# A ternary FFN on Trainium2: the first half group of W1 on ScalarE's queue, quarters for the gathered weights, and two chunks crosswise

## The chip, the cores and the metric

One Trainium2 chip, one of its cores. A core has TensorE (PE, with its weight loads shown apart as PEld), VectorE (DVE), ScalarE (ACT), GpSimd (POOL) and SyncE (SP). They run side by side, each takes its own instructions in order, and they wait for each other by semaphores. DMA queues move data between the device memory and the on-chip memory. The metric is the device time of one execution in microseconds; lower is better.

## The reference

An input `x` of 128 samples, 64 channels and 512 positions is multiplied, sample by sample, by a 64x64 matrix drawn from a table of 200; the result goes through a two-layer network whose weights are made ternary; the output is quantized to 4 bits with one scale for the whole tensor and added to `x`.

```python
def ternarize(W, threshold):                 # threshold 0.05
    absW = jnp.abs(W)
    delta = threshold * jnp.max(absW)
    mask = absW > delta
    n = jnp.maximum(jnp.sum(mask), 1)
    alpha = jnp.sum(jnp.where(mask, absW, 0.0)) / n
    Wt = alpha * jnp.sign(W) * mask
    return W + jax.lax.stop_gradient(Wt - W)

w = weights[conditions]                      # (128, 64, 64) of (200, 64, 64)
c = jnp.einsum('bct,bcd->bdt', x, w)         # "mix": (128, 64, 512)
h = ternary_linear(c, W1, b1)                # 512 -> 2048
h = jax.nn.gelu(h, approximate=False)
y = ternary_linear(h, W2, b2)                # 2048 -> 512
scale = jnp.max(jnp.abs(y)) / 7 + 1e-8
q = jnp.clip(jnp.round(y / scale), -7, 7) * scale
out = x + q
```

Two things set the order at the start: W1's threshold `delta` needs the maximum over the whole of W1 (4 MB), and nothing of layer 1 can be multiplied before it is known.

## The kernel before

**Tiling.** The 128 samples form 16 blocks of 8 samples. A block is four pairs (`PAIRS`), and a pair of samples fills 128 partitions with its 2 x 64 channels; `BLK` = 512 columns of a block are four pairs of 128. Layer 1 has 16 chunks of 128 hidden units (`NH`, index `hc`), layer 2 sums over the same chunks. W1 is held in four groups (`NG`) of four chunks (`GH`), 1 MB each (128 partitions x 2048 float32), in the tiles `nat1[0]` to `nat1[3]`, `nat` in the profile.

**Two parts for each number.** An activation is split into a rounded part in float32r and a rest in float16 (k = 0 and k = 1), and a matrix product runs over both. The ternary weights are held narrow (`terns`, bfloat16) and are widened to float32r by GpSimd (`widen1`, `wf<-terns`) for the first part.

**Program order.** The wrapper `InOrder` (line 36, to which the profile puts almost all instructions) keeps every engine's instructions in the order in which the program writes them. So the order of calls in the source is each engine's queue, and an instruction that waits holds up all that stands behind it on its engine.

**The start, in the order of the source.**

- SP issues all loads: the condition numbers (`first`, 32 KB), W1's pieces by `PIECES` (groups 0 and 1 whole, group 2 in two halves, group 3 in a half and two quarters), x of block 0 in two halves (`load_x(0)`), then b1, W2 (`nat2`), and b2. VectorE makes row numbers (`rows`) of the condition numbers, and GpSimd gathers the table's rows with them: `fetch(n, j)` gathers for block n and pair j into `wg`.
- PE runs 46 matmuls on constants (`idle`) while the loads come in.
- For each piece of W1 VectorE takes the maximum of the absolute values (`top<-nat`). ScalarE makes for groups 0 to 2 the signs (`sign1`) and, in place, the absolute values (`abs1`).
- `place_all(0)`: GpSimd copies all four gathered pairs into the block diagonal matrix `diag` by two instructions, one for each half of the partitions. `place(n, j)` does the same for one pair; later blocks use it.
- `thresholds`: VectorE takes the maximum over the pieces and spreads it, PE turns it across the partitions (`tops_delta_w`), VectorE takes the maximum again and makes `delta1`.
- `mix0(j)` for the four pairs: PE multiplies x by `diag` (`pc<-diag,xt`, eight passes for a pair). `hi0(j)`: ScalarE rounds the result. `lo0(j)`: VectorE makes the rest.
- `mask1`, `signed1` (VectorE): mask and ternary weights of a group; group 0 is done in two halves of two chunks each. Between them stand the four `lo0`.
- `early(hc)`: layer 1's matmuls of block 0 and chunk hc. Chunk 0 is done in two halves of the columns (pairs 0 and 1, then pairs 2 and 3), k = 0 before k = 1 in each; chunk 1 whole. Each chunk has a PSUM bank of its own (`slot`).
- `count1`: PE counts the masks for alpha; `above1` (ScalarE) sums what lies above the threshold.

The passage around the change reads

```python
    mask1(0, parts1[0])
    signed1(0, parts1[0])
    for j in range(2):
        fetch(1, j)
    widen1(0, 0)
    widen1(0, 1)
    for j in range(2, PAIRS):
        fetch(1, j)
    lo0(0)
    ...
    early(0)
    early(1)
    mask1(0, parts1[1])
    signed1(0, parts1[1])
    widen1(0, 2)
    widen1(0, 3)
    abs1(3)
```

After it come, for GpSimd, `widen1(0, 4)`, `widen1(0, 5)`, `place_all(1)`, which reads the gathers of block 1, and `widen1(0, 6)` and further; for PE `count1(0)`, `early(2)`, `early(3)`, the counts of the other groups, `early(4)` and further. From there on block 0's layer 1 and layer 2 run, then blocks 1 to 15.

Of the kernel before, what the change touches and what calls it, by code (L numbers as in the profile page):

```python
# [15 lines left out]
AF = mybir.ActivationFunctionType  # L16
# [23 lines left out]
def tile_cond_ternary_ffn(  # L40
# [12 lines left out]
    pe, act, dve, pool, sp = (  # L53
        InOrder(tc, e) for e in (nc.tensor, nc.scalar, nc.vector, nc.gpsimd, nc.sync)
    )
    B, C, T = x.shape
# [4 lines left out]
    PAIRS = 4  # L61
    BLK = PAIRS * P
    NB = B // (2 * PAIRS)
    NG = 4
    GH = NH // NG
# [44 lines left out]

    nat1, nat2 = [], []

    PIECES = [[slice(0, GH)], [slice(0, GH)], [slice(0, 2), slice(2, GH)]]
    PIECES.append([slice(0, 2), slice(2, 3), slice(3, GH)])
    W1f = W1.rearrange("p k c h -> p k (c h)")
    for g in range(NG):
        w = big.tile([P, GH, T], F32, tag="big", name=f"nat1_{g}")
        for ks in PIECES[g]:
            sp.dma_start(out=w[:, ks, :], in_=W1f[:, g * GH :, :][:, ks, :])
        nat1.append(w)  # L120
    x_next = load_x(0)
    b1t = const.tile([P, NH], F32)
# [1 line left out]
    for g in range(NG):  # L124
        w = big.tile([P, GH, T], F32, tag="big", name=f"nat2_{g}")
# [30 lines left out]
    def half_of(h):  # L156
        return slice(h * C, (h + 1) * C)
# [8 lines left out]
    def fetch(n, j):  # L166

        pair = n * PAIRS + j
        if j == 0:
            gathered[n] = gather.tile([P, PAIRS, D], F32, tag="wg", name=f"wg_{n}")  # L170
        pool.indirect_dma_start(
            out=gathered[n][:, j, :],
            out_offset=None,
            in_=table,
            in_offset=bass.IndirectOffsetOnAxis(ap=rows[:, pair : pair + 1], axis=0),
        )

    def place(n, j):
        for h in range(2):
            out = diag[half_of(h), j, h * D : (h + 1) * D]  # L180
            pool.tensor_scalar(out, gathered[n][half_of(h), j, :], UP, None, ALU.mult)

    def place_all(n):
        for h in range(2):
            out = diag[half_of(h), :, h * D : (h + 1) * D]
            pool.tensor_scalar(out, gathered[n][half_of(h)], UP, None, ALU.mult)
# [3 lines left out]
    def parts(n):  # L190
        return [
            big.tile([P, NT, BLK], t, tag="big", name=f"x{k}_{n}")
            for k, t in enumerate((F32R, F16))
        ]
# [6 lines left out]
    def pair_of(xt, j):  # L201
        return xt[j // 2][:, j % 2, :]

    def mix(xp, j, pc):

        for c in range(NT):
            pe.matmul(
                out=pc[:, c, :],
                lhsT=xp[:, c * P : (c + 1) * P],
                rhs=diag[:, j, :],  # L210
                start=True,
                stop=True,
            )
# [7 lines left out]
    def spread(top1, out, wide_top, space=ps_c, tag="pc"):  # L221

        dve.tensor_copy(wide_top, top1.to_broadcast([P, P]))
        tops = space.tile([P, P], F32, tag=tag, name=f"tops_{out.name}")
        pe.transpose(tops, wide_top, ident_f)
        return tops

    def thresholds(w, top, room):

        top1 = const.tile([P, 1], F32, name=f"top1_{w}")  # L230
        dve.tensor_reduce(top1, top, AX.X, ALU.max)
        delta = const.tile([P, 1], F32, name=f"delta_{w}")
        tops = spread(top1, delta, room)
        yield
        dve.tensor_reduce(delta, tops, AX.X, ALU.max)
        dve.tensor_scalar(delta, delta, THRESHOLD, None, ALU.mult)
        minus = const.tile([P, 1], F32, name=f"minus_{w}")
        dve.tensor_scalar(minus, delta, -1.0, None, ALU.mult)
        yield delta, minus
# [9 lines left out]
    def flat(w):  # L249
        return w.rearrange("p a b -> p (a b)")  # L250


    signs = [big.tile([P, 2, WCH], BF16, tag="big", name=f"signs_{i}") for i in range(2)]
# [3 lines left out]
    above = junk[:, 0, :]  # L257
    top_1 = const.tile([P, sum(map(len, PIECES))], F32)
    sums1 = const.tile([P, NG], F32)

    def group1(tiles, g):
        return tiles[g // 2][:, g % 2, :]

    def sign1(g):
        act.activation(group1(signs, g), flat(nat1[g]), AF.Sign)

    mags = nat1[: NG - 1]

    def abs1(g):

        if g == NG - 1:
            mags.append(big.tile([P, GH, T], F32, tag="big", name="mag"))
        act.activation(flat(mags[g]), flat(nat1[g]), AF.Abs)


    idle = ps_h.tile([P, T], F32, tag="ph", name="idle")
# [6 lines left out]
    for g in range(NG):  # L283
        for ks in PIECES[g]:
            dve.tensor_reduce(
                top_1[:, at : at + 1],
                flat(nat1[g][:, ks, :]),
                AX.X,
                ALU.max,
                apply_absolute_value=True,  # L290
            )
            at += 1
        if g < NG - 1:
            sign1(g)
            abs1(g)
    place_all(0)
    two_next = parts(0)
    pcs = []

    def mix0(j):  # L300
        home, tag = [(ps_c, "pc"), (ps_h, "ph"), (ps_y, "py0"), (ps_y, "py1")][j]
        pc = home.tile([P, NT, P], F32, tag=tag, name=f"pc_0_{j}")
        mix(pair_of(x_next, j), j, pc)
        pcs.append(pc)
# [4 lines left out]
    def lo0(j):  # L309
        part = slice(j * P, (j + 1) * P)  # L310
        dve.tensor_tensor(
            two_next[1][:, :, part], pcs[j], two_next[0][:, :, part], ALU.subtract
        )

    find = thresholds("w1", top_1, first[:, 3, :P])
    next(find)
    delta1, minus1 = next(find)
    for j in range(PAIRS):
        mix0(j)
    hi0(0)  # L320
    hi0(1)
# [1 line left out]
    def mask1(g, part=slice(0, WCH)):  # L323

        dve.tensor_scalar(
            group1(masks, g)[:, part], flat(mags[g])[:, part], delta1, None, ALU.is_gt
        )

    def signed1(g, part=slice(0, WCH)):
        dve.tensor_tensor(  # L330
            group1(terns, g)[:, part],
            group1(masks, g)[:, part],
            group1(signs, g)[:, part],
            ALU.mult,
        )
# [33 lines left out]
    def widen1(n, hc):  # L369

        if n == 0:
            w = w1f[hc % 4]
            g, i = divmod(hc, GH)
            pool.tensor_copy(flat(w), group1(terns, g)[:, i * T : (i + 1) * T])
        else:
            w = w1f[hc % 2]
            pool.tensor_copy(flat(w), w1t[:, hc])
        wide1[n, hc] = w
# [13 lines left out]
    halves = slice(0, HALF), slice(HALF, BLK)  # L392
# [10 lines left out]
                    stop=(c == NT - 1 and k == 1),  # L403
                )

    def layer1_0(n, hc, ph, part=slice(0, BLK), between={}):
        g, i = divmod(hc, GH)
        narrow = group1(terns, g)[:, i * T : (i + 1) * T].rearrange("p (c h) -> p c h", c=NT)
        for k in range(2):
            w = narrow if k else wide1[n, hc]  # L410
            for c in range(NT):
                between.get((k, c), lambda: None)()
                pe.matmul(
                    out=ph,
                    lhsT=w[:, c, :],
                    rhs=cond[n][k][:, c, part],
                    start=(c == 0 and k == 0),
                    stop=(c == NT - 1 and k == 1),
                )
# [80 lines left out]
    ring = [t[:, i, :] for t in rings for i in range(2)]  # L500
    ring += [quarter.tile([P, BLK], F32, tag="quarter", name=f"ring_{i}") for i in (10, 11)]

    def early(hc, between={}):

        slot = (hc + 4) % 6
        if slot < 2:
            ph = ps_h.tile([P, BLK], F32, tag="ph", name=f"ph_0_{hc}")
        else:
            ph = ps_y.tile([P, BLK], F32, tag=f"py{slot - 2}", name=f"ph_0_{hc}")
        for part in halves if hc == 0 else [slice(0, BLK)]:  # L510
            layer1_0(0, hc, ph[:, part], part, between)
        waiting[hc] = ph

    def early_bend(hc):
        if hc % 2 == 0:
            pairs0[hc // 2] = big.tile([P, 2, 2, BLK], F32R, tag="big", name=f"h_{hc}")
        two = [pairs0[hc // 2][:, hc % 2, k, :] for k in range(2)]
        on_pool = hc in (0, 2, 4, 6)
        bend(0, hc, waiting.pop(hc), two, ring[hc % len(ring)], pool if on_pool else None)
# [79 lines left out]

    mask1(0, parts1[0])  # L600
    signed1(0, parts1[0])
    for j in range(2):
        fetch(1, j)
    widen1(0, 0)
    widen1(0, 1)
    for j in range(2, PAIRS):
        fetch(1, j)
    lo0(0)
    lo0(1)
# [1 line left out]
    hi0(3)  # L611
    lo0(2)
    lo0(3)
    early(0)
    early(1)
    mask1(0, parts1[1])
    signed1(0, parts1[1])
    widen1(0, 2)
    widen1(0, 3)
    abs1(3)  # L620
    for g in range(NG):
        above1(g)
# [66 lines left out]
    for hc in range(NH - LAG):  # L689
# [13 lines left out]
        if hc in (5, 7, 9, 11):  # L703
            j = (hc - 5) // 2
# [191 lines left out]
    order = [*range(AWAY, NB - 2), *range(AWAY), NB - 2]  # L896
# [212 lines left out]
    while s < len(steps):  # L1109
        n, hc = steps[s]  # L1110
# [10 lines left out]
    n = NB - 1  # L1121
# [108 lines left out]
```

## Time and profile before

| | |
|---|---|
| median of 3 runs | 963.38 us (963.26 to 963.51) |
| the profiled execution | 963.14 us |
| its span, first to last instruction | 961.4 us |
| PE busy | 949.9 us (99%) |
| VectorE, ScalarE, GpSimd busy | 708.3, 637.0, 705.3 us |
| granted TensorE clock | 0.999 |
| read from and written to the device memory | 46.44 and 32.51 MB |

A PE that is busy for 99% of the span includes the 46 matmuls on constants (2.96 to 14.91 us), which compute nothing that is needed. A view by line says little here, because all instructions stand at line 36; the names of the tiles tell them apart. The first 45 us, in order of time, are what bears on the change. The landing of a transfer is its issue time plus the time from issue to landing that the view of a tile gives: the numbers land at 2.5 us, group 0 at 6.0, group 1 at 8.5, x's first half at 15.7.

### The profile page before, as it was taken

To read this page: it belongs to the slowest core of one execution; us is meant where nothing else is said; L and a number is where in the kernel's file an instruction comes from. 1 tells how busy PE (TensorE), PEld (TensorE's weight loads), DVE (VectorE), ACT (ScalarE), POOL (GpSimd) and SP (SyncE) were. 2 spreads that over 40 slices of the span, in tenths; PEclk is the share of its full clock that TensorE was granted. 3 is DMA by queue.
4 is the path that set the end of the run, shared out by engine and by line. 5 is a ranking of instruction groups with operands and counts; after the bars stand their busy time and mean duration, and the time that the engine had idled before them with its cause. 6 is when DMAs were issued, how large, how long until landed. Compare 5 with 4: busy or idle time off the path is not lost.

```text
span 961.4 us, 17574 instructions
## 1 busy us (share of the span) xinstructions
PE 949.9 (99%) x6072; PEld 739.3 (77%) x6072; DVE 708.3 (74%) x1239; ACT 637.0 (66%) x1148; POOL 705.3 (73%) x1060
## 2 busy tenths in 40 slices
PE   8999999999999999999999999999999999999997
PEld 4687667888788788788878778788878878878784
DVE  7999766666676766666676676666667798888986
ACT  7995446656656666665666656666565777878784
POOL 6866867677686776767767686776767879788872
PEclk9999999999999999999999999999999999999999
DMA  9301011110111100111010111100131184575751
GB/s 359 103 23 47 14 33 49 32 61 15 35 49 34 60 24 25 52 41 49 25 70 15 34 50 33 59 25 25 49 121 60 47 305 172 186 239 170 277 204 61
DMA packets 33195, 80.11 MB, mean 83 GB/s; under 512 B 3792, under 2 KB 3792, under 8 KB 30160
## 3 DMA queue, kind: packets, MB, share of 16 engines
q1 hardware_dynamic: 31056, 76.86, 22.7%
q0 software_dynamic: 2048, 2.10, 0.7%
q8 instruction: 49, 0.80, 0.3%
q14 instruction: 42, 0.34, 0.1%
HBM read 46.44 MB, written 32.51 MB: 82 GB/s over the span
## 4 chain that ended last, share of the span: by engine, by line
PE 96%; DVE 2%; DMA 1%; ACT 1%; issue 0%; POOL 0%; SPq 0%; ACTq 0%
PE py L36 47%; PE xy L36 22%; PE z L36 16%; PE pc L36 6%; PE ph L36 6%; DVE top L36 1%; DMA nat<-in_L_ffn_W 1%; DVE xt L36 0%; DVE y_last L36 0%; ACT diag L36 0%; POOL wf L36 0%; PE number L36 0%; DVE y L36 0%; ACT h L36 0%; ACT ring L36 0%
## 5 line engine op out<-in xcount | busy, mean ns | idle before, releaser
L36 PE MATMUL py<-wf,h 128*128 128x512 f32 x1088 | 316.5, 416 | 0.7 <-DVE y L36 0.6
L36 POOL CAST wf<-w2t 128x512 fp32r<-128x512 fp8e4 x240 | 229.6, 977 | 105.2 <-PE py L36 102.1
L36 POOL CAST wf<-sums 128x256 fp32r<-128x256 fp8e4 (+1 forms) x336 | 183.0, 550 | 86.1 <-PE xy L36 82.3
L36 PEld LDWEIGHTS py<-wf,h 128*128 128x128 f32 x1088 | 196.6, 189 | 45.1 <-POOL wf L36 0.8
L36 DVE SCALAR_TENSOR_TENSOR low_parts<-ring,h 128x512 f16<-128x512 f32 x228 | 202.1, 924 | 39.3 <-ACT h L36 39.3
L36 PE MATMUL py<-w2t,low_parts 128*128 128x512 fp8e4 x920 | 218.6, 379 | 0.0
L36 ACT ACTIVATE ring<-ring,b1t,alpha_up 128x512 f32<-128x512 f32 x216 | 175.2, 818 | 58.8 <-DVE ring L36 53.9
L36 DVE TENSOR_TENSOR ring<-xy,ring 128x256 f32<-128x256 f32 x216 | 119.8, 555 | 119.3 <-PE xy L36 119.3
L36 ACT COPY ring<-xy 128x256 f32<-128x256 f32 x216 | 80.5, 373 | 171.7 <-PE xy L36 171.2
L36 PEld LDWEIGHTS <-low_parts 128*128 128x128 f16 x920 | 89.6, 97 | 84.5 <-issue 0.3
L36 ACT ACTIVATE h<-ring 128x512 fp32r<-128x512 f32 x232 | 133.9, 626 | 0.6
L36 POOL CAST wf<-w1t 128x256 fp32r<-128x256 fp8e4 (+1 forms) x240 | 131.3, 563 | 2.5 <-PE xy L36 0.3
L36 PE MATMUL xy<-xb,wf 128*128 128x256 f32 x448 | 98.8, 302 | 0.0
L36 PE MATMUL xy<-xt,wf 128*128 128x256 f32 x448 | 88.1, 277 | 0.1
L36 PE MATMUL xy<-xl,sums 128*128 128x256 f16 x448 | 87.9, 278 | 0.0
L36 PE MATMUL xy<-xl,w1t 128*128 128x256 f16 x448 | 86.8, 275 | 0.0
L36 PE MATMUL z<-xl,sums 128*128 128x256 f16 x448 | 85.5, 273 | 0.0
L36 PEld LDWEIGHTS xy<-xt,wf 128*128 128x128 f32 x448 | 76.2, 188 | 10.2 <-issue 0.2
L36 PEld LDWEIGHTS xy<-xb,wf 128*128 128x128 f32 x448 | 75.9, 189 | 10.2
L36 PEld LDWEIGHTS <-sums 128*128 128x128 fp8e4 x896 | 69.3, 97 | 14.8
L36 POOL DMA_INDIRECT wg<-in_L_cond_weights,rows x64 | 63.9, 998 | 18.2 <-issue 8.6
L36 PEld LDWEIGHTS <-w1t 128*128 128x128 fp8e4 x736 | 61.6, 98 | 18.0 <-issue 4.3
(134 smaller groups left out, 1349.3 us busy)
## 6 DMA issues: line engine op xcount, KB each, us to landing
xt<-in_x SPq DMA_DIRECT2D x36, 512.0 KB, 5.6
y_dram<-y SPq DMA_DIRECT2D x15, 1024.0 KB, 4.3
out<-xt SPq DMA_DIRECT2D x30, 512.0 KB, 3.4
x_quarters<-in_x SPq DMA_DIRECT2D x56, 256.0 KB, 2.7
nat<-in_L_ffn_W SPq DMA_DIRECT2D x6, 1024.0 KB, 10.2
y_back<-y_dram SPq DMA_DIRECT2D x2, 1024.0 KB, 7.4
nat<-in_L_ffn_W SPq DMA_DIRECT2D x3, 512.0 KB, 8.7
wg<-in_L_cond_weights,rows POOLq DMA_INDIRECT x64, 2.5
```

Of the source, the lines that this page charges most:

```text
L36: return lambda *args, **kw: self._tc.keep_in_program_order(make(*args, **kw))
```

## The change

- W1's group 0 comes in two halves. The first is issued from ScalarE's queue, as ScalarE's first instruction; SP issues the second after the numbers. VectorE's maximum, `sign1` and `abs1` of group 0 are done by halves (both signs, then both absolute values).
- `place_all(0)` becomes four `place(0, j)`: eight instructions, two behind each gather, for two.
- `mix0(0)` moves ahead of the threshold's transpose on PE; pairs 1 to 3 stay behind it.
- `early(0)` and `early(1)` become `early_two()`: chunk 1 also in two halves of the columns, and the eight sets of four matmuls in a crosswise order, in which chunk 0's second half, k = 1, comes after chunk 1's first half. `early` no longer splits chunk 0, and the choice of the bank is a function of its own.
- On GpSimd one `fetch` of block 1 instead of two stands ahead of the first two widenings, two stand behind them, and `fetch(1, 3)` moves behind `widen1(0, 3)`.

```diff
-    PIECES = [[slice(0, GH)], [slice(0, GH)], [slice(0, 2), slice(2, GH)]]
+    PIECES = [[slice(0, 2), slice(2, GH)], [slice(0, GH)], [slice(0, 2), slice(2, GH)]]
...
-        for ks in PIECES[g]:
-            sp.dma_start(out=w[:, ks, :], in_=W1f[:, g * GH :, :][:, ks, :])
+        for i, ks in enumerate(PIECES[g]):
+            queue = act if g == 0 and i == 0 else sp
+            queue.dma_start(out=w[:, ks, :], in_=W1f[:, g * GH :, :][:, ks, :])
...
-            sign1(g)
-            abs1(g)
-    place_all(0)
+            pieces = PIECES[g] if g == 0 else [slice(0, GH)]
+            for ks in pieces:
+                sign1(g, ks)
+            for ks in pieces:
+                abs1(g, ks)
+    for j in range(PAIRS):
+        place(0, j)
...
     find = thresholds("w1", top_1, first[:, 3, :P])
+    mix0(0)
     next(find)
     delta1, minus1 = next(find)
-    for j in range(PAIRS):
+    for j in range(1, PAIRS):
         mix0(j)
...
-    def layer1_0(n, hc, ph, part=slice(0, BLK), between={}):
+    def layer1_0(n, hc, ph, part=slice(0, BLK), between={}, ks=range(2)):
...
-        for k in range(2):
+        for k in ks:
...
+    def early_two():
+
+        phs = [bank(hc) for hc in range(2)]
+        order = [(0, 0, 0), (0, 0, 1), (0, 1, 0), (1, 0, 0), (1, 0, 1), (0, 1, 1)]
+        for hc, h, k in order + [(1, 1, 0), (1, 1, 1)]:
+            layer1_0(0, hc, phs[hc][:, halves[h]], halves[h], ks=(k,))
...
-    for j in range(2):
-        fetch(1, j)
+    fetch(1, 0)
     widen1(0, 0)
     widen1(0, 1)
-    for j in range(2, PAIRS):
+    for j in range(1, 3):
         fetch(1, j)
...
-    early(0)
-    early(1)
+    early_two()
     mask1(0, parts1[1])
     signed1(0, parts1[1])
     widen1(0, 2)
     widen1(0, 3)
+    fetch(1, 3)
     abs1(3)
```

In `order` a triple is chunk, half of the columns, part k.

## The prediction

> **What bounds the kernel now.** I read the busy shares first, then busy time by stretch, then the chain of waits over the start, then each engine's timeline there. Busy time by stretch (columns: stretch and length, PE, PEld, DVE, ACT and POOL busy with counts, granted clock, DMA share, GB/s):
>
> ```profile
> 14.90:24.30 9.40, 8.12 (x75) 6.95 (x74) 8.51 (x16) 8.79 (x10) 7.68 (x9) 1.00 1.03 408
> 24.30:38.00 13.70, 13.70 (x106) 8.81 (x107) 12.87 (x13) 12.29 (x15) 12.74 (x13) 1.00 0.24 95
> 38.00:80.00 42.00, 42.00 (x204) 32.22 (x203) 40.62 (x37) 39.76 (x45) 25.84 (x24) 1.00 0.13 39
> 80.00:940.00 860.00, 859.26 (x5569) 677.19 (x5568) 622.90 (x1141) 557.64 (x1062) 649.29 (x996) 1.00 0.23 78
> ```
>
> From 24.30 on PE is never without work until the last stage, which is untouched. So the change is worth just what it moves the moment when chunk 2 starts (`early(2)`, 24.29), plus any stall it opens behind it. Who sets 24.29, by the chain of waits (start, length, what):
>
> ```profile
> 1.66 6.83 DMA nat<-in_L_ffn_W
> 8.51 6.86 DVE top L36 x6
> 15.93 0.33 PE tops_delta_w L36
> 16.26 3.60 PE pc L36 x32
> 19.88 0.60 ACT x L36
> 20.50 0.69 DVE x L36
> 21.19 0.67 DVE masks L36
> 21.88 0.70 DVE terns L36
> 22.64 1.61 POOL wf L36
> 24.29 3.88 PE ph L36 x16
> ```
>
> W1's group 1 lands (8.49), VectorE finds the maxima, PE turns them, mixes four pairs, then ScalarE rounds the last pair, VectorE takes its rest, then makes the second half of group 0's ternary, and GpSimd widens chunk 2. VectorE's own timeline over that stretch shows how little of this is slack:
>
> ```profile
> 16.30 0.29 DVE L36 TENSOR_REDUCE delta_w<-tops_delta_w 128x1 f32<-128x128 f32 x1 [0.42 <-PE tops_delta_w L36]
> 18.29 2.00 DVE L36 TENSOR_TENSOR x<-pc,x 128x512 f16<-128x512 f32 x3
> 20.50 0.69 DVE L36 TENSOR_TENSOR x<-pc,x 128x512 f16<-128x512 f32 x1 [0.20 <-ACT x L36]
> ```
>
> From 16.30 VectorE works without a break to 22.57, but for 0.20 waiting for ScalarE's last rounding. So a second chain, VectorE's own, lies only 0.20 under the chain through the mixes. Freeing the mixes alone yields at most 0.20.
>
> **Part 1, the load on ScalarE's queue.** Before, SP issues the numbers at 0.74 and group 0 at 1.19. Busy time by stretch again (same columns):
>
> ```profile
> 1.70:2.20 0.50, 0.00 (x0) 0.00 (x0) 0.15 (x1) 0.49 (x2) 0.40 (x2) 1.00 0.30 66
> 2.20:3.20 1.00, 0.24 (x1) 0.10 (x1) 0.60 (x2) 0.04 (x1) 0.71 (x2) 1.00 1.01 197
> 3.20:4.20 1.00, 1.00 (x4) 0.29 (x3) 0.68 (x3) 0.00 (x0) 0.00 (x0) 1.00 0.93 385
> 4.20:14.20 10.00, 10.00 (x42) 4.32 (x41) 7.97 (x6) 7.69 (x5) 4.20 (x5) 1.00 1.02 400
> ```
>
> W1's bytes begin about 1.0 us after issue, run at half rate for 1 us, then at 385 to 400 GB/s: a saturated stream, so all landings shift together by s. ScalarE's first instruction also starts at 0.74 (its table load); a DMA in that place starts the stream 1.19 - 0.74 = 0.45 earlier. No ScalarE-queue DMA is in the trace. Lower bound s = 0: the table load (1.28) comes first, the issue falls to 2.02, after SP's own 1.19, and nothing starts sooner. Upper bound: two queues also fill the slow stretch (1.0 us at 197 instead of 400 GB/s loses 0.5), s = 0.95. I take 0.45, nearest to the issue rows. The Trainium skill speaks against more: "DMA: Bandwidth & Descriptors", "Issuing engines are not separate DMA queues", says that loads started by different engines run on the same 16 DMA engines, and that a second issuer saves only the time to issue. By that rule s is 0.45 and the 0.95 falls away; the 197 GB/s row cannot say whether the slow start belongs to a queue or to the engines.
>
> The issue itself costs ScalarE 0.3 to 0.5 (SP's rows), before its table load and a dummy Gelu that nothing awaits; its first real work came at 6.00. The numbers now share the engines with 0.5 MB (1.3 us at 400 GB/s): they land 0 to 1.3 later than 2.53, `rows` is ready by 5.3 at worst instead of 3.97, the gathers land by 11.5 to 15.1 instead of 10.2 to 13.8 (first: issue 4.26 plus 5.9; last: 8.24 plus 5.6). VectorE reduces group 0 in two halves from 5.3 at worst, 2 x 1.14 (the 1024-column form), done by 7.6, while group 1 lands at 8.49 - 0.45 = 8.04. All hidden; without the 0.4 of cover the excess would go straight into the chain. The maxima then end at 8.04 + 0.02 + 6.86 = 14.92, the transposed input is ready at 15.43 instead of 15.88.
>
> **Part 2, the halves on ScalarE.** Two instructions more. A cast of 512 columns takes 0.58, one of 2048 columns 1.91: about 0.14 fixed, so a half is near 1.02 and both splits add 0.23. ScalarE's wait of 0.48 for VectorE before `abs1(0)` goes, and it starts earlier, so it is free for `hi0(0)` near 16.9 (17.69 before), and pair 0 is mixed at 16.3. Hidden.
>
> **Part 3, placing by quarters.** Eight instructions of 64x64 (362 to 368 ns where undisturbed) for two of 0.86 to 0.90: 2.9 us for 1.79, but six of them run between gather landings. The last two end 0.74 behind the last gather, 14.6 to 15.9, against pair 3's mix near 18.2. Hidden. The fetch of the next block that GpSimd issues before the first widening is now one (1.0) for two, which leaves it free at 17.2 at the latest.
>
> **Part 4, `mix0(0)` ahead of the transpose.** PE runs in order, so the threshold now waits for pair 0's mix, and this for x's first half. That was issued at 4.84 and took 10.8:
>
> ```profile
> L36 SPq DMA_DIRECT2D xt<-in_x x1: 487/487/487, 4.8 to 4.8; - x1
> ...
> DMA to landing us min/median/max: 10.8/10.8/10.8
> ```
>
> It landed at 15.65; now 15.65 - s. Then 0.05 to start, eight passes at 0.112 (32 in 3.74, the last 0.28 long) make 0.89, and from the transpose's start to VectorE is 0.37: 15.20 + 0.05 + 0.89 + 0.37 = 16.51, where it was 16.30. **The threshold comes 0.21 later**, although its input is 0.45 sooner: queued behind the mix are the transpose and thus all of VectorE's masks. In return the mixes end at 16.3 + 24 x 0.112 = 19.0 instead of 19.68, and `hi0(3)` at 19.8 instead of 20.46, so VectorE's wait of 0.20 is gone. Net for `lo0(3)` and all behind it: (16.96 - s) - 16.30 - 0.20 = **0.46 - s**, that is +0.01.
>
> **Part 5, crosswise chunks.** Chunk 1 in halves is 8 matmuls of 256 columns more and 8 of 512 fewer. A half chunk takes 0.93 (19.59 to 20.52), a whole one 1.81 (31.18 to 32.99): +0.1 in all. PE starts at 19.25 (first widening, 0.21 later), runs 3.7 with no wait for `lo0(3)` (ready 21.2, wanted 21.6), and count 0.4: done at 23.4. Chunk 2 waits for its widening at 24.25 anyway: the cover is 0.85, and the 0.1 is nothing, as is the 0.15 which PE lost to `lo0(3)` before.
>
> **Part 6, `fetch(1, 3)` behind `widen1(0, 3)`.** GpSimd's queue:
>
> ```profile
> 21.09 0.95 POOL L36 DMA_INDIRECT wg<-in_L_cond_weights,rows  x1 [0.30 <-issue]
> 22.64 6.25 POOL L36 CAST wf<-terns 128x512 fp32r<-128x512 bf16 x4 [0.60 <-DVE terns L36]
> 28.86 2.74 POOL L36 TENSOR_SCALAR diag<-wg 64x256 f32<-64x256 f32 x2
> ```
>
> It was issued in idle time; now 1.25 lies between the second and third of four widenings of 1.6 each. Chunk 4's ends at 28.7 (PE wants it at 29.2), chunk 5's at 30.2 (wanted 31.2). Then `place_all(1)`, 1.75 without VectorE beside it, then chunk 6's at 32.6 (32.3 before; wanted 32.96). Hidden by 0.3, if the gather has landed by 30.5. From its issue at 26.1, the rows bound it: 2.5 (median of all) gives 28.6, 6.4 (the longest of the first eight) 32.5. The stream that slowed it ends at 13.79 + 15.4 = 29.2, b2 at 29.8, less s; I take 30.0 and no stall. At 32.5 `place_all(1)` and chunk 6's widening (0.62) end at 34.95, and the stall is 2.0.
>
> **Sum.** Chunk 2: +0.21 - 0.20 = +0.01; other parts 0. The profiled execution took 963.14 (span 961.4 and 1.7 around it), so 963.15; the median of the runs stands 0.24 above it, and I forecast on it: **963.4**. Its own range, s from 0.2 to 0.7: 963.1 to 963.7.
>
> **Rivals.**
> A, a late gather (slower): place GpSimd's `place_all(1)`; it decides from a landing past 30.5, each us later costing one, 2.0 at most. For it: 5.3 to 6.4 in the rows of the stream. Against: the stream ends before. Time 963.4 + 2.0 = 965.4.
> B, the two queues fill the slow start: s = 0.95, chunk 2 at -0.5, 962.9. For it: half rate for a whole us after a single queue's first big load. Against: DMA share is 1.01 in that stretch, so the engines were occupied.
> C, the load does nothing for the stream (the table load first, or numbers and half group merely swap places): s = 0, +0.46, 963.9. For it: the table load sits at 0.74 today. Against: no DMA needs a table.
>
> **How the numbers follow.** Forecast 0.52, A 0.18, B 0.14, C 0.16. Range 962.7 to 965.2: from B less the runs' scatter of 0.2 to nearly A's full price. 0.2% is 1.93 us, about what a measurement of this kernel can tell from no change. Upward (965.3) only A at its full price passes it, or A in part together with C, half of A's chance: 0.09; nothing worked out here reaches 961.5, so 0.03 for what I don't see; within: 0.88.
>
> **What would show it.** s: group 1's maxima start at 8.05 instead of 8.51. Part 4: VectorE's threshold reduction at 16.5, behind eight mix passes on PE. The net: chunk 2 at 24.3, with PE idle some 0.8 before it. Part 6: GpSimd idle or not before `place_all(1)`, and PE without a gap near 33. I am wrong if the threshold comes earlier than 16.1 or later than 17.0, or if PE has a gap after chunk 2.

## The result and the profile after

The changed kernel takes **964.93 us** (964.72 to 966.62), beside 963.41 for the kernel before in runs of the same kind: 1.52 us more, ratio 1.0017 with a 95% interval of 1.0011 to 1.0024. That is inside the range and, by its median, within the 0.2% that was called no change; the interval excludes no difference at all and reaches a little over the 0.2%. The profiled execution took 965.1 us, its span is 963.3, the granted clock 0.998.

Most of the difference arises in the first 32 us. Matmul by matmul, PE is 0.63 us later than before at chunk 2 (24.92 for 24.29), 1.34 at chunk 4, 1.40 at chunk 5 (32.58 for 31.18) and 1.51 at 84 us. The rest comes later: 1.61 at 111 us, and 2.02 from 630 us on. The last 0.41 of this arises near 613 us, where two of VectorE's instructions (`low_parts`) take 2.52 instead of 1.71. The chain of waits of the changed kernel over the start (start, length, what) does not run through W1 any more:

```profile
5.02 10.65 DMA xt<-in_x
...
15.80 1.13 PE pc L36 x8
...
19.13 2.39 DVE x L36 x4
21.52 0.67 DVE masks L36
...
24.14 2.35 DVE terns L36
26.49 3.59 DVE masks L36 x2
...
30.13 0.55 PE number L36 x16
```

Now x's first half sets the threshold, through pair 0's mix, and from there the chain is VectorE's alone, down to the mask of group 3 for which PE waits at 30.13. The waits of PE between 15 and 940 us (waiting line and what it waited for: us in total, times, longest):

```profile
PE pc L36 <- DMA xt<-in_x: 0.9, 1, 0.9
PE ph L36 <- POOL wf L36: 0.9, 1, 0.9
...
PE number L36 <- DVE masks L36: 0.6, 1, 0.6
```

The first is the wait of the early mix. The second stands before chunk 0 (20.72 for 19.59). The third is the gap behind chunk 2 that the prediction named as its refutation.

**What the load did.** The numbers, by the view of their tile (issue, then us from issue to landing), in the changed kernel:

```profile
L36 SPq DMA_DIRECT2D first<-in_itok_B x1: 391/391/391, 0.7 to 0.7; - x1
...
DMA to landing us min/median/max: 3.3/3.3/3.3
```

They take 3.3 us where they took 1.8. And the stream gained nothing: group 1 lands at 8.49 and x's first half at 15.66, as before (8.49 and 15.65). In the five other kernels below that have this load the stream even lost: VectorE begins group 1's maxima at 9.12 to 9.52, and at 8.51 to 9.00 in the eight without it. ScalarE did issue its load early (0.74 to 1.15, ahead of its table load), and the first packet of that load runs at 1.84; but SP's first packet of W1 now runs at 3.70 instead of 2.24. What one queue won, the other lost. With the numbers 1.54 later, the gathers land at 11.7 to 15.0 instead of 10.2 to 13.8.

**What the quarters did.** GpSimd's timeline of the changed kernel (start, busy, what, count, and in brackets the idle time before and what ended it):

```profile
11.83 0.38 POOL L36 TENSOR_SCALAR diag<-wg 64x64 f32<-64x64 f32 x1 [1.33 <-DMA wg<-in_L_cond_weights,rows]
15.14 3.49 POOL L36 TENSOR_SCALAR diag<-wg 64x64 f32<-64x64 f32 x7 [2.94 <-DMA wg<-in_L_cond_weights,rows]
18.90 1.11 POOL L36 DMA_INDIRECT wg<-in_L_cond_weights,rows  x1 [0.27 <-POOL diag L36]
...
22.65 1.57 POOL L36 DMA_INDIRECT wg<-in_L_cond_weights,rows  x1 [0.30 <-issue]
24.23 1.17 POOL L36 CAST wf<-terns 128x512 fp32r<-128x512 bf16 x2
25.56 2.25 POOL L36 DMA_INDIRECT wg<-in_L_cond_weights,rows  x1 [0.16 <-issue]
27.80 1.18 POOL L36 CAST wf<-terns 128x512 fp32r<-128x512 bf16 x2
```

One quarter comes behind its own gather. The second, pair 0's upper half of the partitions, waits until 15.14, behind the last landing (15.0), and seven of eight instructions run after it; in the built program the wait ahead of this instruction names the other three gathers too. In all six kernels with this order it starts 0.1 to 0.3 behind the last landing. Placing ends at 18.63 instead of 15.80, the fetch that follows at 20.01, and only then come the widenings for chunk 0.

**What the fetches did.** The last four rows show two fetches of 1.57 and 2.25 us, where the kernel before needed 0.95 to 1.07, and behind each of them two widenings at 0.58 us apiece, where the kernel before needed 1.6 for each (its four in 6.25 us). VectorE's timeline beside them, in the changed kernel, over the product of group 1 and the masks of groups 2 and 3:

```profile
24.14 2.35 DVE L36 TENSOR_TENSOR terns<-masks,signs 128x2048 bf16<-128x2048 bf16 x1
26.41 1.27 DVE L36 TENSOR_SCALAR masks<-nat,delta_w 128x2048 bf16<-128x2048 f32 x1
27.61 2.46 DVE L36 TENSOR_SCALAR masks<-mag,delta_w 128x2048 bf16<-128x2048 f32 x1
```

and the same three instructions in the kernel before:

```profile
23.81 1.51 DVE L36 TENSOR_TENSOR terns<-masks,signs 128x2048 bf16<-128x2048 bf16 x1
25.24 1.63 DVE L36 TENSOR_SCALAR masks<-nat,delta_w 128x2048 bf16<-128x2048 f32 x1
26.80 1.63 DVE L36 TENSOR_SCALAR masks<-mag,delta_w 128x2048 bf16<-128x2048 f32 x1
```

Read together, the two engines take turns. Undisturbed, a mask takes 1.27. The fetch at 25.56 stands still beside the mask at 26.41 (0.97 + 1.27 = 2.24, it took 2.25) and the mask loses nothing. Then the two widenings behind it run in a row, and the mask at 27.61 stands still for both (1.27 + 1.18 = 2.45, it took 2.46). In the kernel before, widenings and VectorE alternate, and each of VectorE's instructions loses about 0.35. The product at 24.14 stands still in the same way for the two widenings behind the fetch of 1.57 (1.2 + 1.17 = 2.37, it took 2.35). So a fetch that VectorE has held up makes VectorE pay 1.18 for two widenings where alternating costs 0.7: about 0.5 for each such fetch. Fetches at this place that took only 1.18 to 1.22 (mix_first_alone, no_act_queue, mix_behind below) were followed by widenings that alternate. Why VectorE gets no turn between the two widenings behind a longer one, no run shows. From the end of the last rest to the copy of the count VectorE needs 9.81 us, where it needed 8.70.

### The profile page after: what moved, and what is told of

It reads as the page before. It is cut to its first block, busy times and chain, and to the rows that moved or that the text cites. A ratio compares the mean times of both kernels' runs of the same rounds, so it can differ in the third digit from the quotient of the medians.

```text
span 963.3 us, 17602 instructions
## 1 busy us (share of the span) xinstructions
PE 950.8 (99%) x6080; PEld 740.1 (77%) x6080; DVE 709.0 (74%) x1240; ACT 636.9 (66%) x1150; POOL 706.4 (73%) x1066
## 4 chain that ended last, share of the span: by engine, by line
PE 94%; DVE 3%; DMA 1%; ACT 1%; issue 1%; SPq 0%; ACTq 0%; DVEq 0%
PE py L36 46%; PE xy L36 21%; PE z L36 16%; PE pc L36 6%; PE ph L36 5%; DMA xt<-in_x 1%; DVE masks L36 1%; SPq L36 0%; ACT ring L36 0%; DVE terns L36 0%; DVE y L36 0%; DVE xt L36 0%; DVE y_last L36 0%; DVE low_parts L36 0%; DVE x L36 0%
## 5 line engine op out<-in xcount | busy, mean ns | idle before, releaser
L36 PEld LDWEIGHTS xy<-xb,wf 128*128 128x128 f32 x448 | 75.9, 189 | 10.2
```

The costliest lines, as they stand in the source:

```text
L36: return lambda *args, **kw: self._tc.keep_in_program_order(make(*args, **kw))
```

## The experiments

All times of one row come from one profiled execution, but for the median and its ratio to the kernel before (963.31 to 963.41 beside them). "Window" is VectorE's time from the end of its last rest (`lo0(3)`) to the copy of the count (left out for the last three kernels, whose rests stand elsewhere), "alpha" the start of the instruction that makes alpha.

| kernel | threshold | chunk 0 | chunk 2 | window | alpha | median us | ratio, 95% |
|---|---|---|---|---|---|---|---|
| before | 16.30 | 19.59 | 24.29 | 8.70 | 31.32 | 963.41 | |
| changed | 17.07 | 20.72 | 24.92 | 9.81 | 32.72 | 964.93 | 1.0017 [1.0011, 1.0024] |
| act_queue_alone | 17.25 | 24.14 | 28.84 | 8.71 | 35.86 | 967.10 | 1.0037 [1.0023, 1.0050] |
| quarters_alone | 16.43 | 20.61 | 24.77 | 9.20 | 31.90 | 964.32 | 1.0010 [1.0001, 1.0019] |
| mix_first_alone | 17.25 | 20.04 | 24.81 | 8.71 | 31.85 | 963.91 | 1.0006 [0.9997, 1.0015] |
| fetch_order_alone | 16.42 | 19.72 | 24.42 | 9.19 | 31.89 | 963.78 | 1.0004 [0.9995, 1.0013] |
| no_act_queue | 17.32 | 20.32 | 25.09 | 9.19 | 32.56 | 964.77 | 1.0015 [1.0006, 1.0024] |
| upper_once | 19.15 | 23.18 | 27.88 | 9.19 | 35.35 | 967.78 | 1.0048 [1.0035, 1.0062] |
| mix_behind | 17.08 | 22.27 | 26.97 | 9.19 | 34.45 | 966.38 | 1.0031 [1.0020, 1.0042] |
| fetches_mid | 18.01 | 21.69 | 25.89 | 8.70 | 32.88 | 971.45 | 1.0078 [1.0064, 1.0091] |
| fetches_late | 18.20 | 21.88 | 26.08 | 8.71 | 33.06 | 973.04 | 1.0101 [1.0086, 1.0116] |
| rests_last | 16.56 | 19.86 | 24.05 | | 31.58 | 973.14 | 1.0106 [1.0090, 1.0121] |
| rests_last_2 | 16.73 | 20.03 | 24.22 | | 31.75 | 964.62 | 1.0013 [1.0004, 1.0022] |
| rests_last_3 | 16.39 | 19.69 | 24.06 | | 31.05 | 964.23 | 1.0009 [1.0000, 1.0018] |

### The parts alone

**act_queue_alone**: the kernel before with Part 1 and Part 2.

```diff
...
+            queue = act if g == 0 and i == 0 else sp
+            queue.dma_start(out=w[:, ks, :], in_=W1f[:, g * GH :, :][:, ks, :])
...
```

> The kernel before, with W1's first half group on ScalarE's queue and group 0's signs, absolute values and maxima in halves; nothing else. Theory 1 (what ScalarE's queue costs is the numbers: they land 1.5 later, so the gathers end near 15.0 and the two placing instructions at 16.9 instead of 15.8): the four mixes run from 16.9 to 20.5, the last rounding and the last rest come 0.8 later, chunk 2 starts at 25.1, 964.2. Theory 2 (the load itself is harmless, the loss of the whole change sits in the placing by quarters): 963.4. A stream that starts sooner would show x's first half landing before 15.5; I expect 15.65.

It cost the most of all parts, 3.76 us. The numbers landed at 5.0, 2.5 later than without the second queue, and the four pairs were placed only at 18.86. W1 and x came 1.0 later too in this execution. Then something that no theory had: busy time by stretch (columns as before: PE, PEld, DVE, ACT, POOL, clock, DMA share, GB/s)

```profile
18.90:20.70 1.80, 1.78 (x10) 1.78 (x10) 0.44 (x1) 0.00 (x0) 1.26 (x2) 0.61 1.00 414
20.70:22.50 1.80, 1.80 (x10) 1.80 (x10) 0.69 (x1) 0.65 (x2) 1.75 (x3) 0.50 1.04 432
```

PE had idled for 2.54 and 1.70 us around the transpose, its granted clock fell to 0.61 and 0.50, and a mix pass took 0.21 instead of 0.11: the 32 passes took 5.47 instead of 3.74. So some 1.7 of the 3.76 is the clock. One of the five executions took 965.89 at a mean granted clock of 0.999, the others 967.07 to 967.88 at 0.996 or 0.997.

**quarters_alone**: the kernel before with four `place(0, j)` for `place_all(0)` (Part 3).

```diff
-    place_all(0)
+    for j in range(PAIRS):
+        place(0, j)
```

> The kernel before, with place(0, j) four times instead of place_all(0); nothing else. Theory 1 (the first instruction for the upper 64 partitions waits for all four gathers, and seven of the eight follow the last landing): GpSimd is done near 17.4 instead of 15.8, its two fetches end at 20.1, the first widening runs from 20.2 instead of 18.5, PE idles 1.0 after the mixes, the fetches behind it fall into VectorE's masks: chunk 2 at 25.0 or later, 964.2 to 964.9. Theory 2 (each pair is placed behind its own gather): GpSimd done at 14.7, nothing lost, 963.4 or less.

GpSimd's timeline of this run:

```profile
9.73 0.38 POOL L36 TENSOR_SCALAR diag<-wg 64x64 f32<-64x64 f32 x1 [0.55 <-DMA wg<-in_L_cond_weights,rows]
...
14.08 3.03 POOL L36 TENSOR_SCALAR diag<-wg 64x64 f32<-64x64 f32 x7 [3.98 <-DMA wg<-in_L_cond_weights,rows]
```

The same picture without the late numbers: one quarter early, seven in a row behind the last landing, done at 17.11 instead of 15.79. PE waits 0.64 for chunk 0, and one fetch slides beside VectorE (window 9.20). It costs 0.98: alpha is 0.58 later, and the 0.41 near 613 us, which the changed kernel and no_act_queue have too, comes on top. The kernels with `place_all(0)` do not have it.

**mix_first_alone**: `mix0(0)` ahead of the transpose (Part 4).

```diff
+    mix0(0)
     next(find)
     delta1, minus1 = next(find)
-    for j in range(PAIRS):
+    for j in range(1, PAIRS):
```

> The kernel before, with pair 0's mix ahead of the threshold's transpose; nothing else. Theory 1 (PE's order puts the threshold behind the mix, which waits for the placing at 15.8 and x at 15.65): VectorE's threshold reduction at 17.1 instead of 16.3, 0.2 of it won back at the last rest, chunk 2 at 24.9, 964.0. Theory 2 (VectorE's chain has slack): 963.4 or less.

The threshold comes at 17.25, 0.95 later; 0.43 of it is won back, because the four rests now run in a row, in 2.48 where they took 2.90 with the wait of 0.20, and chunk 2 and alpha are 0.52 and 0.53 later. The median is 0.57 up; its interval includes no difference.

**fetch_order_alone**: the new places of `fetch(1, 1)` to `fetch(1, 3)` (Part 6).

```diff
...
     widen1(0, 3)
+    fetch(1, 3)
     abs1(3)
```

> The kernel before, with one fetch of block 1 ahead of the first widening, two behind the second, the last behind the fourth; nothing else. Theory 1 (a fetch that runs beside VectorE's masks and ternary products costs VectorE time, as its product of group 1 took 2.35 instead of 1.51 after the whole change): VectorE's count copy comes 0.3 to 0.8 later, the third group's count waits on PE, 963.7 to 964.2. Theory 2 (only the queue's length counts, and it has room): PE has no gap, 963.4.

Chunk 2 is where it was (+0.13, of which 0.12 is already in the threshold), but the pattern of the changed kernel is there once. GpSimd's timeline:

```profile
26.07 2.24 POOL L36 DMA_INDIRECT wg<-in_L_cond_weights,rows  x1
28.31 1.17 POOL L36 CAST wf<-terns 128x512 fp32r<-128x512 bf16 x2
```

The fetch stands beside VectorE's mask (1.27, undisturbed), the two widenings run in a row, and VectorE's product of group 2, begun at 28.11, takes 2.47. PE waits 0.2 for the count, and alpha is 0.57 later with the window 0.49 longer. GpSimd waited 0.55 for the gather before `place_all(1)`, but PE has no gap from it. The median is up by 0.44; its interval includes no difference.

### Taking parts away

**no_act_queue**: the changed kernel with all of W1 on SP and group 0 whole.

```diff
...
-            queue = act if g == 0 and i == 0 else sp
-            queue.dma_start(out=w[:, ks, :], in_=W1f[:, g * GH :, :][:, ks, :])
+            sp.dma_start(out=w[:, ks, :], in_=W1f[:, g * GH :, :][:, ks, :])
```

> The changed kernel with all of W1 again on SP's queue, group 0 whole; its quarters, its mix ahead, its crosswise chunks and its order of fetches stay. Theory 1 (the half group on ScalarE's queue delays the numbers and with them GpSimd's whole start; the other parts, made for that lateness, still cost something): the numbers land at 2.6 instead of 4.1, the gathers at 13.8 instead of 15.0, GpSimd places until 17.2 instead of 18.6, PE starts chunk 0 near 19.8 instead of 20.7; the threshold stays at 17.1, since x's first half sets it, and the fetch among the widenings stays: 964.3. Theory 2 (the queue is harmless): 964.9.

The numbers landed at 2.5 again, placing ended at 17.08, chunk 0 came 0.40 earlier than in the changed kernel and one fetch fewer lay in the window (9.19). But x was late in this execution (PE waits 1.34 for it), the threshold came at 17.32, and alpha is only 0.16 earlier. Of the 1.52 in the medians 0.16 went away too. Within the whole change the load costs about nothing more, though alone it costs 3.76.

**upper_once**: the changed kernel with the lower halves by quarters and all upper halves in one instruction.

```diff
     for j in range(PAIRS):
-        place(0, j)
+        place(0, j, [0])
+    pool.tensor_scalar(diag[C:, :, D:], gathered[0][C:], UP, None, ALU.mult)
```

> The changed kernel, with the lower 64 partitions placed by quarters, each behind its own gather, and the upper 64 by one instruction for all four pairs. Theory 1 (seven of the eight quarters stand behind the last gather and make GpSimd late): GpSimd is done at 16.1 instead of 18.6, PE starts chunk 0 near 19.9 instead of 20.7 without waiting for the widening; the threshold comes 0.3 later, as the first mix waits for 16.1 instead of x's 15.7: 964.4 to 964.7. Theory 2 (GpSimd's lateness at the start is made good before it matters): 965.2.

The four lower halves ran at 13.07, 14.04, 15.62 and 16.47, each behind its own gather: by pairs works as long as no instruction for the upper partitions stands between. But now pair 0 is complete only with all others, at 17.79, PE idles for 3.52 before its first mix, the threshold queued behind it is at 19.15, and the clock halves (0.50 from 20 to 22 us). 4.5 us over the kernel before.

**mix_behind**: the changed kernel with all mixes behind the transpose again.

```diff
-    mix0(0)
     next(find)
     delta1, minus1 = next(find)
-    for j in range(1, PAIRS):
+    for j in range(PAIRS):
```

> The changed kernel, with pair 0's mix behind the threshold's transpose again. Theory 1 (the threshold's 0.8 is what VectorE's chain loses at the start): the threshold at 16.3, the last rest at 21.2 instead of 21.5, everything on VectorE 0.3 earlier: 964.6. Theory 2 (GpSimd's lateness rules and the threshold has slack): 964.9. If PE's clock falls while it idles from 15 to 16 or longer, the mixes stretch and the time exceeds 964.9.

It is 1.45 us slower than the changed kernel (the medians), though its threshold is as early. PE idles 1.69 before the transpose, and the clock is 0.56 from 17.0 to 18.8 and 0.50 from 18.8 to 20.6, while in the changed kernel it is 1.00 from 15.7 to 19.9. In the changed kernel's profile PE idles for only 0.89 there. But W1 was later here too (group 1's maxima from 9.35), and with it the transpose, and so was placing (gathers to 16.4), because the numbers landed at 4.9. So this run does not give a clean price for the place of the mix, and that the early mix is what keeps the clock is not shown.

### Moving the fetches away

**fetches_late** and **fetches_mid**: the changed kernel with `fetch(1, 1)` to `fetch(1, 3)` out of the window, behind chunks 7, 9 and 11 (`place_all(1)` behind 13), and behind chunks 6, 7 and 9 (`place_all(1)` behind chunk 2 of layer 2).

```diff
+        if hc in [6, 7, 9]:
+            fetch(1, 1 + [6, 7, 9].index(hc))
```

> The changed kernel, with block 1's last three fetches moved behind chunks 7, 9 and 11, and its placing behind chunk 13, all long before they are used. Theory 1 (fetches beside VectorE's masks and products hold VectorE up): the product of group 1 takes 1.5 instead of 2.35, the count no longer waits for the last mask (0.58), and what is left is the late start of chunk 0: 964.0. Theory 2 (VectorE was slow for another reason): 964.9.

> The changed kernel, with block 1's last three fetches behind chunks 6, 7 and 9, where VectorE only takes maxima, and its placing behind chunk 2 of layer 2, where GpSimd was idle. Theory 1 (a fetch beside VectorE's masks and products holds VectorE up): the product of group 1 takes 1.5 instead of 2.35, no count waits for a mask, and chunk 2's start, 0.6 late by the late widening, is what remains: 964.0 to 964.2, and no wait of PE for GpSimd behind chunk 6. Theory 2 (the fetches among the widenings cost nothing): 964.9.

Both confirm the head: window 8.70 and 8.71, products 1.51, masks 1.63, no wait before the count. (Their thresholds are later, 18.01 and 18.20, with x; chunk 2 follows the threshold by 7.88, as in the changed kernel by 7.85.) Both lose more further on. The waits of PE in fetches_mid:

```profile
PE py L36 <- POOL wf L36: 3.1, 1, 3.1
...
PE tops_delta_w L36 <- DVE junk L36: 0.8, 1, 0.8
```

The 3.1 is `place_all(1)` (3.56 us) ahead of a widening of layer 2. The 0.8 is W2's threshold, late because VectorE's product of group 3 takes 2.70 instead of 1.22: the moved fetches have pushed GpSimd's queue so that a widening is running when the product begins, and the widening and the sum behind it (0.63 and 1.30, undisturbed) go first. In the kernel before, the product began 0.03 ahead of that sum, and the sum had to wait (2.32). In fetches_late widenings cost PE 1.8 and 3.4. Behind these waits the clock fell as well, to 0.50 from 66 to 72 us in fetches_mid and to 0.57 from 60 to 64 us in fetches_late. So no kernel here shows the fetches out of the window and the gain kept to the end.

### Looking for something better

**rests_last**, **rests_last_2**, **rests_last_3** start from the kernel before, with the crosswise chunks, the rests of pairs 2 and 3 behind the second half of group 0's ternary, and the fetches partly or all moved behind chunks 6 and later. The second takes the sums for alpha at chunk 5; the third has `abs1(3)` earlier and another crosswise order.

```diff
-    lo0(2)
-    lo0(3)
-    early(0)
-    early(1)
     mask1(0, parts1[1])
     signed1(0, parts1[1])
+    lo0(2)
+    lo0(3)
+    early_two()
```

> The kernel before, with chunks 0 and 1 crosswise and, since the crosswise order bears it, the rests of pairs 2 and 3 behind the second half of group 0's ternary; block 1's fetches and placing go behind chunks 7 to 13, and the ternary of group 2 behind alpha. Theory 1 (chunk 2 starts when VectorE has made group 0's second half and GpSimd has widened it undisturbed): chunk 2 starts at 23.9 instead of 24.3, PE then waits for nothing but alpha's sums from ScalarE: 962.9 to 963.2. Theory 2 (VectorE's work only changes places, and ScalarE's sums hold alpha where it was): 963.4.

> The kernel before, with chunks 0 and 1 crosswise, the rests of pairs 2 and 3 behind the second half of group 0's ternary, ScalarE's sums taken up at the start of chunk 5 instead of amid chunk 4, two fetches of block 1 behind chunks 6 and 7 and its placing behind chunk 2 of layer 2. Theory 1 (ScalarE's sums held alpha in the run before, and the moved fetches and placing cost the rest): chunk 2 at 23.8, chunk 5 at 30.7 instead of 31.2, then chunk 6 waits some 0.2 for its bank: 963.0 to 963.2. Theory 2 (moved fetches collide again): over 964.

> As the run beside it, but ScalarE takes group 3's absolute values ahead of the rounding of pairs 2 and 3, which fills its idle 0.55, the sums stay amid chunk 4, and the crosswise order takes chunk 1's first half ahead of chunk 0's second. Theory 1: chunk 2 at 24.05 (PE waits 0.25 for the rounding of pair 3), alpha 0.5 earlier, no wait behind: 963.1. Theory 2 (moved fetches collide again): over 964.

All three gain at the head: chunk 2 at 24.05, 24.22 and 24.06 for 24.29, with thresholds 0.26, 0.43 and 0.09 later. All lose it further on. rests_last pays 1.5 and 5.3 us of PE waiting for widenings behind all four fetches and the placing, and the clock falls there too. The other two are 0.2 to 0.3 ahead of the kernel before at chunk 5 (relative to the threshold in rests_last_2, absolutely in rests_last_3) and lose it at W2's threshold, for which PE waits 1.07 and 0.81, because of the same group-3 product (2.69 and 2.71 us). None beats the kernel before. The head of rests_last_3 with the fetches at their old place was not tried, nor was the crosswise order alone.

## Why the prediction was right, and where it was not

**The total** lies inside the range and, by its median, inside the 0.2% called no change. It was 1.5 us low all the same, and outside the 963.1 to 963.7 that the sum gave itself. The account behind it was wrong: both signs that the prediction named against itself came, the threshold at 17.07 (later than 17.0) and a gap of PE behind chunk 2. That the range holds the result is luck: its upper end was priced for rival A, which did not come. Three steps are wrong, two of them behind the word "hidden".

**Part 1, s = 0.45: mis-sized, s = 0 in this profile.** This is rival C's number; the five other kernels with the load show a stream that comes later, not sooner. Group 1's maxima start at 8.52, not 8.05. The bound from below had the right outcome by the wrong cause: the table load did not come first, but the second half of group 0 on SP's queue started 1.46 later. The Trainium skill, "DMA: Bandwidth & Descriptors", "Issuing engines are not separate DMA queues", grants a second issuer the issue time alone; the runs show not even that arriving at W1's end. Numbers "0 to 1.3 later" came 1.5 later here, and 2.2 to 2.6 in the other runs with this load. "Hidden" held for the rows, not for what the late gathers do to Part 3.

**Part 4: the mechanism right, its sizes a little off.** With s = 0 the step says 16.96 for the threshold and +0.46 net; measured 17.07 and +0.34 at the last rest's end (21.52 for 21.19), and +0.52 alone. VectorE's wait of 0.20 vanished as worked out. Two small errors partly cancel: the mix started 0.14 behind x's landing, not 0.05, and 0.43 was won back, not 0.20.

**Part 3: failed.** "Six of them run between gather landings" was wrong: one did. The step took the wait of each instruction for that of its own pair; the upper half's covers all gathers. Placing ended 18.63, not 14.6 to 15.9, and GpSimd was free at 20.0, not 17.2. That moved `fetch(1, 2)` into VectorE's window; `fetch(1, 3)` is there by Part 6.

**Part 6: the place was right, the mechanism wrong.** The gather of `fetch(1, 3)` landed in time: GpSimd waited 0.83 for it, but began `place_all(1)` at 29.81, ahead of the 30.5 that the part allowed, and PE has no gap at chunk 6, so rival A did not decide. What costs is the turn: "1.25 between two widenings" took 2.25, and afterwards VectorE stands still for two widenings. The window fits a count: no pair of widenings in a row behind a held-up fetch, 8.70 to 8.71 (five kernels); one, 9.19 to 9.20 (five); two, 9.81 (the changed kernel). About 0.5 us for each. In fetch_order_alone the one fetch is Part 6's own; in quarters_alone it is Part 3's delay. The Trainium skill, "SBUF — State Buffer", "SBUF: two separate sides", says of the port pair that VectorE and GpSimd share that, for a VectorE instruction in a two-port mode or with two inputs in that memory, whoever starts first holds it for the whole instruction and the other blocks. The rows of 2.25 and 2.46 agree on whole instructions, each the sum of its own work and the other's. On who goes first they do not, by the starts in the profile: the fetch of 25.56 stood still for a mask of 26.41, and the mask of 27.61 for widenings from 27.80 on. The prediction read GpSimd's queue for lateness only, not for what it runs beside.

**Part 5: about right, its gain not shown.** The two chunks take 3.78 to 3.80 in the six kernels with this crosswise order, 3.90 in the kernel before with its wait for a rest, and 3.76 in quarters_alone, where the old order met no wait. Its cover of 0.85 was gone, since chunk 0 started 1.13 later: chunk 2 begins at 24.92 without a gap, behind PE's own run. Part 2 was hidden: ScalarE was free at 16.55 and waited for pair 0 until 16.96.

**The sum as measured:** +0.34 at the last rest (Part 4 with s = 0) and +1.11 in the window (two fetches) make +1.45; the copy of the count came 1.44 later, chunk 5 1.40, the median 1.52. The profiled executions differ by 1.96, with what came behind chunk 5, so that the sum meets the median this closely is partly chance. The parts alone add to 3.76 + 0.98 + 0.57 + 0.44 = 5.75 us, and for two of them the interval includes no difference: they are not additive. Alone, the load starves PE before the mixes and the clock falls; in the changed kernel's profile it stays at 1.00. Two of that kernel's 17 executions took 966.52 and 966.62 at a mean clock of 0.996, the others had 0.998 or 0.999; that these two had such a fall is likely, but they have no trace. What remains open is why the numbers landed at 4.1 in the changed kernel's profile and at 4.7 to 5.1 in the other five with the same load.

## What to carry to other kernels

An operation that is "hidden" on its own engine is not free until one has looked at which instructions of the other engines it runs beside: here a DMA issue moved on GpSimd cost VectorE 0.5 us, and VectorE was the bound. A large load put on another queue to start early takes its bytes from the small load on which a chain of gathers hangs. And work split so as to run as its inputs come helps only if each piece waits for its own input: look at what the wait names before counting on it.

## What the runs showed of the hardware

- **A pause of PE can halve its clock, and its length alone does not decide.** PE idle for 1.69 us (mix_behind), 2.54 and 1.70 (act_queue_alone) and 3.52 (upper_once) was followed by a granted clock of 0.50 and passes of 0.21 instead of 0.11 us, for 3.4 us; 0.89 (the changed kernel), 1.54 (quarters_alone), 1.58 (fetches_mid) and even 2.53 (fetches_late) before the mixes were not. In the clock records of the traces every fall begins a whole number of 3.41 us behind the first record: 3 of them in mix_behind, 4 in act_queue_alone and upper_once, 15 in rests_last, 16 in fetches_late, 17 in fetches_mid. That fits a decision every 3.41 us over the stretch just ended: the 2.53 lies across two stretches, 1.53 in one and 1.00 in the next, and the clock held; 2.02 within one (upper_once) brought it down. The limit is an estimate, near 1.7: 1.70 within one stretch (fetches_late, near 51 us) held, 1.69 and a single transpose (mix_behind) did not. The Trainium skill, "TensorE: Matmul & The Clock Gate", "Part 1: The HAM clock gate", puts the fall behind an idle window of about 3.4 us; here less idle time was enough.
- **GpSimd and VectorE take turns by whole instructions:** a fetch took 0.95 to 1.0 alone and 2.24 to 2.25 beside a mask of 1.27; two widenings took 1.17 when they went in a row, and the mask or product beside them 2.35 to 2.47; alternating, a widening took 1.6 and a mask 1.63. A start 0.03 us ahead or 0.25 behind decided whether the group-3 product took 1.22 or 2.71 us.
- **Two queues did not deliver sooner than one:** with two, group 1 landed at the same time in the changed kernel (8.49) and 0.6 to 1.0 us later in five others, and 32 KB landed 1.5 to 2.6 us later.
